# A graph layer on one core: who copies the counts, where the first nodes are kept, one relu for a copied group, and 105 copied groups in place of 104

## The chip, the core and the metric

The kernel runs on one core of a Trainium2 chip. The metric is the device time of one launch in microseconds (us), and lower is better. A core has five engines that run side by side, each through its own instructions in order: PE (matrix products), DVE (vector operations), ACT (activations and copies), POOL (here it only issues gathers) and SP (here it only issues transfers). They wait for each other by semaphores. SBUF is the working memory, PSUM the small memory that PE writes its results to; transfers to and from HBM run on 16 DMA engines.

## The reference

One layer of message passing on a graph with 12,500 nodes of 64 features and 200,000 edges of 32 features, sorted by destination, all in f32:

```python
msg_in = concat([nodes[row], nodes[col], edge_features])       # row: source, col: destination
messages = relu(msg_in @ mW1 + mb1) @ mW2 + mb2
aggregated = segment_sum(messages, col, num_segments=12500)
upd_in = concat([nodes, aggregated])
out = layernorm(x + relu(upd_in @ uW1 + ub1) @ uW2 + ub2)      # over the 64 features
```

## The kernel before

**Tiles, groups, supers, ranges.** A tile is 128 edges; there are 1563. Six tiles are a group `s` (261 of them), two groups a super `g` (131 of them). The edges are sorted, so the destinations of a tile lie in a window of 32 nodes. Groups are gathered into 34 ranges `u` of nodes; for each range PE sums into one PSUM tile `sums` (hidden features of up to 480 nodes) and one PSUM row `cnt` (how many edges each node has, since mb2 enters once for each edge). There are two buffers of `sums`, but one of `cnt`.

**Prologue.** Products of the nodes with the two node parts of mW1 are made once and stored as tables: `tab_a` (source part) and `tab_b` (destination part with mb1).

**One iteration of the main loop** (lines 763 to 831) handles group `s`, with pieces of its neighbours. Its order is written out by hand, and each engine takes its instructions in that order:

- POOL: `gather` (line 217) fetches the source rows of `tab_a` for a later group, 128 rows in one indirect DMA. A buffer `xg` is free again when the add of the group that had it is done; nine are in turn.
- SP: `windows` (lines 276 to 285) reads window starts and fetches rows of `tab_b` into `rhs`.
- `node_part(s)` (line 380): DVE adds the gathered rows to the PSUM tile `pc` (lines 397 and 401), ACT takes the relu (398, 399 and 402) into `h`. `pc` and `h` have two buffers each.
- `joined(s, 0, ...)`: the first part of DVE's column copies (below).
- the update of an earlier range, one stage an iteration: `evacuate` (ACT), `statistics` (DVE), `deviation` (ACT), `norm` (DVE).
- `collect(s - 1)` (line 412): PE adds the counts of the group before (line 431), then its hidden features (line 434). At the first group of a range it first clears `sums` (409) and `cnt` (429).
- `close(u)` (line 445), at the end of a range: ACT copies `cnt` into row 0 of `xw` (line 448) and `sums` into `sums_s` (line 449). PE then reads both: `carry` (442, 443) takes the overlap of 32 nodes over into the next range, `update` (471, 472) makes the node update.
- `select(g + 1)` (line 236), in every second iteration: DVE computes `node` (line 243), the first node of each tile's window against the partition number, into the PSUM tile `cps`; compares the destinations in `l` with it, which turns them into 0 and 1 (line 245); and makes `sel`, a tile's edges against its 32 nodes (line 251). `l` is the weight with which PE spreads the rows of `rhs` over the edges; `cps` also holds `slot`, the numbers 0 to 31.
- `edge_part(s + 1)` (line 363): PE makes `pc` of the next group from `l` and `rhs` (line 374).
- `rest(s)`: pieces of the prologue that are put into the first iterations.
- `joined` again, then `singly` (the column copies on ACT).

**Copied groups.** In 104 of the groups, two of the six tiles are not gathered. Their source columns are instead copied one by one out of `xtop` and `xbot`, which hold all nodes' features, into a tile `xc`: 64 of its 128 columns by ACT (line 345) and 64 by DVE (line 352), at addresses that the engine's sequencer loads eight at a time (line 322). PE then multiplies `xc` with mW1 (line 377). `PACE` (line 74) says how many groups are copied for each group of progress, and so which ones (`COPIED`); the copies of one are spread over the iterations before it, some 26 to 28 columns an iteration on each of the two engines. In a copied group, DVE adds the four gathered tiles from `pc` into `h`, ACT takes their relu in `h`, and a second ACTIVATE takes the relu of the other two tiles straight from `pc`.

`wh`, the input of line 243, is fetched in two parts by `halves` (line 537): the columns of the first eight supers before the loop, the others in `rest(2)`.

Of the kernel before, what the change touches and what calls it, by code (L numbers as in the profile page):

```python
# [10 lines left out]
F32 = mybir.dt.float32  # L11
I32 = mybir.dt.int32
AF = mybir.ActivationFunctionType
ALU = mybir.AluOpType
# [3 lines left out]
P = 128  # L18
# [7 lines left out]
SUP = 12  # L26
NSUP = -(-NT // SUP)
# [3 lines left out]
WIN = 32  # L31
# [15 lines left out]
UW = UN + WIN  # L47
# [23 lines left out]
U8 = mybir.dt.uint8  # L71
YBASE = XBASE + 4 * XCOLS
LEAD = 8
PACE = ((11, 0.413), (50, 0.44), (130, 0.424), (261, 0))
FINAL = 258


def progress(s):

    return sum(r * max(0, min(s + 1, b) - a) for (a, r), (b, _) in zip(PACE, PACE[1:]))  # L80

# [9 lines left out]
def updates():  # L91


    def node(s):
        return N * min(1.0, s * SUB * P / E) ** 2
    at = [0]
    for s in range(1, NSUB):
        if s > at[-1] and node(s + 1) - node(at[-1]) > UN - WIN:
            at.append(s)
    at = [a for a in at if a < NSUB - 32]  # L100
    steps = -(-(NSUB - 3 - at[-1]) // 4)
    return at + [at[-1] + -(-(NSUB - 3 - at[-1]) * (i + 1) // steps) for i in range(steps)]


UPD = updates()

UL = min(UB * P, -(-int(N * (1 - (UPD[-1] * SUB * P / E) ** 2) + WIN // 2) // 64) * 64)


@with_exitstack  # L110
def gnn_kernel(ctx: ExitStack, tc: tile.TileContext, x1T, x, eT, e_rows, src, src_row, dst, dst_row, wlist, wrow, wnext, whalf,
# [24 lines left out]
    nc = tc.nc  # L136
# [21 lines left out]
    xw = [const.tile([P, UB * P], F32, name=f"xw{k}") for k in range(2)]  # L158
# [17 lines left out]
    pidx = const.tile([P, 1], F32, name="pidx")  # L176
# [1 line left out]
    zero_b = const.tile([P, UW], BF, name="zero_b")  # L178

    cpool = ctx.enter_context(tc.tile_pool(name="cpsum", bufs=1, space=bass.MemoryType.PSUM))  # L180
    cps = cpool.tile([P, WIN + SUP], F32, name="cps")
    slot = cps[:, :WIN]
    drc = const.tile([P, NT], F32, name="drc")
    flag_i = const.tile([1, 1], I32, name="flag_i")
# [3 lines left out]
    wh = const.tile([P, NTP // 2], I32, name="wh")  # L188
# [11 lines left out]
    def tiles(s):  # L200
        return range(s * SUB, min((s + 1) * SUB, NT))
# [20 lines left out]
    with tc.tile_pool(name="sup", bufs=2) as sup, tc.tile_pool(name="work", bufs=2) as work, tc.manual_schedule():  # L222
# [3 lines left out]
        def loadd(g):  # L226
# [6 lines left out]
                nc.sync.dma_start(l[q:q + WIN].bitcast(I32), dv[:, b].broadcast_to([WIN, SUP // 2, P]))  # L233
            L[g] = l

        def select(g, at=None):


            nt = min(SUP, NT - g * SUP)
            l = L[g]  # L240
            c = WIN + SUP // 2 * (g % 2)
            node = cps[:, c:c + SUP // 2]
            nc.vector.tensor_scalar(node, wh[:, g * SUP // 2:(g + 1) * SUP // 2], pidx, None, op0=ALU.add)
            for r in ([slice(0, P)] if g > 2 else [slice(q, q + WIN) for q in SK]):
                nc.vector.tensor_tensor(l[r], l[r].bitcast(I32),  # L245
                                        node[r].unsqueeze(2).broadcast_to([r.stop - r.start, SUP // 2, P]),
                                        op=ALU.is_equal)
            if at is not None:
                joined(at, 1, 3)
            s = sup.tile([P, SUP, WIN], F32, name="sel")  # L250
            nc.vector.tensor_tensor(s[:, :nt], slot.unsqueeze(1).broadcast_to([P, nt, WIN]),  # L251
                                    drc[:, g * SUP:g * SUP + nt].unsqueeze(2).broadcast_to([P, nt, WIN]),
                                    op=ALU.is_equal)
            S[g] = s

        def counts(g):

            SB[g] = S[g].bitcast(BF).rearrange("p k (w h) -> p k w h", h=2)
# [88 lines left out]
        def joined(s, part, of):  # L347

            todo = [(o, k, ACTS + e) for o, k, lo, hi in portion(s, P - ACTS) for e in range(lo, hi, 2)]
            for o, k, a, m in share(todo, part, of):  # L350
                for e, top, bot in addresses(k, a, m, ET.DVE):
                    nc.vector.tensor_tensor(o[:, e:e + 1].bitcast(I32), top.bitcast(I32), bot.bitcast(I32),  # L352
                                            op=ALU.bitwise_or)
# [26 lines left out]
        def node_part(s):  # L380

            n = len(tiles(s))
            pc = pcs.pop(s)
            h = work.tile([P, 2, SUB // 2, DH], F32, name="h")
            if s < XG:
                xt = xs.pop(s)
                for i in range(n):
                    k, b = divmod(i, 2)
                    q = 64 * b
                    nc.tensor.matmul(pc[:, b, k, :], xt[q:q + 64, k, :], w1a[q:q + 64], start=False,  # L390
                                     stop=i + 2 >= n)
                nc.scalar.activation(h, pc, AF.Relu)
            else:
                a = xg.pop(s)[0].rearrange("p (b k) f -> p b k f", b=2)
                if s in COPIED:
                    m = SUB // 2 - 1
                    nc.vector.tensor_tensor(h[:, :, :m], pc[:, :, :m], a[:, :, :m], op=ALU.add)  # L397
                    nc.scalar.activation(h[:, :, :m], h[:, :, :m], AF.Relu)  # L398
                    nc.scalar.activation(h[:, :, m:], pc[:, :, m:], AF.Relu)
                for b, m in parts(n) if s not in COPIED else []:  # L400
                    nc.vector.tensor_tensor(h[:, b, :m], pc[:, b, :m], a[:, b, :m], op=ALU.add)  # L401
                    nc.scalar.activation(h[:, b, :m], h[:, b, :m], AF.Relu)  # L402
            hs[s] = h
# [41 lines left out]
        def close(u):  # L445

            ps, pn = sums.pop(u)
            nc.scalar.copy(xw[u % 2][0:1, :UW], pn)
            nc.scalar.copy(sums_s[u % 2], ps)

        us = {}
# [1 line left out]
        def width(u):  # L453

            return UN if u + 1 < K else UL

        def blocks(u):
            return UB if u + 1 < K else -(-UL // P)

# [109 lines left out]
        def zeros(i, n):  # L569

            w = XCOLS // n
            for t in (xtop[D:], xbot[:D]):
                nc.scalar.activation(t[:, i * w:(i + 1) * w], ident[:D, 0:1].broadcast_to([D, w]), AF.Copy, scale=0.0)
# [80 lines left out]
        for k, c in enumerate(range(0, NB, NCH)):  # L654
            chunk_a(c)
            if k == 0:
                chunk_b(0, [B0v, Bv])
            if k == 2:

                w0 = wint[:, :GE * SUP // SUB * LS]  # L660
                nc.vector.tensor_scalar(past, w0[:, GE * SUP // SUB * LS - 1:], float(EARLY - WIN), None, op0=ALU.is_gt)
                nc.vector.tensor_scalar(w0, w0, float(EARLY - WIN), None, op0=ALU.min)
                windows(0)
                windows(1)
            if k == 4:
                relative(0, 8 * SUP)
            if k == 6:
                offsets()
            if k == 9:
                select(0)  # L670
                load(0)
                counts(0)

        def rest(s):

            if 3 <= s < 9 and s % 2:
                others((s - 3) // 2 * 4, (s - 3) // 2 * 4 + 4)
            if 3 <= s < 11:
                zeros(s - 3, 8)
            if s == 9:  # L680
                columns_list()
            if s == 1:
                relative(8 * SUP, 8 * SUP + WCH)
            elif s == 2:
                relative(8 * SUP + WCH, NT)
                halves(4 * SUP, NTP // 2)
            elif s == BS:
                nc.sync.dma_start(wa, wrow.rearrange("o (p c) -> (o p) c", c=NSUP))
                nc.sync.dma_start(wb, wnext.rearrange("o (p c) -> (o p) c", c=NSUP))
                nc.scalar.dma_start(w2, mW2)  # L690
                nc.scalar.dma_start(u1a, uW1[D:2 * D, :])
                nc.scalar.dma_start(b2c, mb2.rearrange("(f o) -> f o", o=1))
                nc.vector.memset(uz[:D], 0.0)
                nc.vector.memset(ux[:D], 0.0)
                nc.vector.memset(eps, EPS)
                nc.vector.memset(ones, 1.0)
                nc.vector.tensor_copy(ux[D:], ident[D:, D:])
                nc.scalar.dma_start(uz[D:], uW1[0:D, :])
                nc.scalar.dma_start(ux[ONE:ONE + 1], ub2.rearrange("(o f) -> o f", o=1))
                nc.scalar.dma_start(ub1_s, ub1.rearrange("(f o) -> f o", o=1))  # L700
                nc.scalar.dma_start(u2, uW2)
            elif s == BS + 2:
                weights()
                checks()
# [14 lines left out]
        def checks():  # L719
# [23 lines left out]
            nc.vector.tensor_scalar(gap[:, :K - 1], gap[:, :K - 1], float(UN), None, op0=ALU.is_gt)  # L743
            nc.vector.tensor_scalar(gap[:, K - 1:K], gap[:, K - 1:K], float(min(UN, UL)), None, op0=ALU.is_gt)
            nc.vector.tensor_copy(gap[:, K:], past)
# [17 lines left out]
        for s in range(last + 2):  # L763
            g, j = divmod(s, SUP // SUB)
# [71 lines left out]
    with tc.If(flag > 0), tc.tile_pool(name="gen", bufs=1) as up:  # L836
# [28 lines left out]
        with tc.For_i(0, NT, 1) as t:  # L865
# [26 lines left out]
            pc = psum.tile([P, DH], F32, name="pcg", tag="pc")  # L892
# [4 lines left out]
            h = up.tile([P, DH], F32, name="hg")  # L897
# [6 lines left out]
            m = up.tile([P, 1], F32, name="m")  # L904
# [97 lines left out]
```

## Time and profile before

| | |
|---|---|
| three runs | 2490.05, 2479.22 and 2493.46 us; median 2490.05 |
| the profiled execution | 2486.88 us, of which the span (first to last instruction) is 2485.1 us |
| clock granted to PE | 0.535 of full speed in the mean |
| DMA | 191.63 MB, mean 77 GB/s |
| 300 to 2440 us of the span: busy | PE 1459.59, DVE 1030.77, ACT 1517.72, POOL 1139.42 us of 2140 |
| gathers (line 217) | 1355, of 944 ns each |
| adds (lines 397, 401) | 104 of 690 ns (four tiles), 146 of 958 ns (six tiles) |

The profile is one execution. A row of a group of instructions gives the line of the kernel, the engine, what is written and read, how many there are, their busy time together and the mean duration of one; then how long the engine sat idle before them, and what ended that: an instruction of another engine, a transfer, "issue" (nothing that the profile shows), or "remote" (a semaphore whose sender it can't tell). The waits are the same idle times, summed by who waited for whom: total, number, longest. Idle time of one engine matters only as far as it delays the end.

### The profile page before, as it was taken

The numbers are of one execution on the slowest core, as the hardware profiler recorded it, in microseconds if no ns is written. First come the engines' busy times: TensorE is split into PE (matmuls) and PEld (weight loads), VectorE is DVE, ScalarE is ACT, GpSimd is POOL, SyncE is SP. The second block draws the span as 40 slices with busy tenths as digits, with TensorE's granted clock in tenths as the row PEclk, the third lists the DMA queues.
The fourth block names the chain that finished last, engine by engine and source line by source line (L and its number), as shares of the span: only waits on it lengthen the run. The fifth ranks groups of instructions, "written<-read, shape, count | busy, mean of one in ns | idle before, by whom it ended". The sixth has DMA issues, their size and how long they took to land. (4 is left out here: it accounts for less than half of the span.)

```text
span 2485.1 us, 47640 instructions
## 1 busy us (share of the span) xinstructions
PE 1630.3 (66%) x9652; PEld 1392.7 (56%) x9652; DVE 1118.3 (45%) x7843; ACT 1612.1 (65%) x7232; POOL 1280.4 (52%) x1364
## 2 busy tenths in 40 slices
PE   1238575666566666666567666776667777777878
PEld 1237465655555555555555555555556656666666
DVE  0211554544444544445444444544544444544544
ACT  0015676767777767768776766776767776777754
POOL 7153455555555555545555555555555555555540
PEclk7565555555555555555555555555555555555556
DMA  5343232322222222222222222222222222222222
GB/s 131 104 120 84 71 91 78 89 78 71 69 67 65 74 64 72 68 68 72 71 71 75 76 69 74 78 75 76 74 75 73 75 78 79 76 77 74 80 72 53
DMA packets 207229, 191.63 MB, mean 77 GB/s; under 512 B 57243, under 2 KB 173297, under 8 KB 206945
## 3 DMA queue, kind: packets, MB, share of 16 engines
q0 software_dynamic: 43360, 86.92, 13.7%
q1 hardware_dynamic: 149040, 92.72, 13.5%
q10 hardware_dynamic: 14546, 8.93, 1.3%
q8 instruction: 91, 1.49, 0.3%
q14 instruction: 192, 1.57, 0.2%
HBM read 170.65 MB, written 17.76 MB: 76 GB/s over the span
## 5 line engine op out<-in xcount | busy, mean ns | idle before, releaser
L217 POOL DMA_INDIRECT xg<-tab_a,src_s x1295 | 1222.6, 944 | 1120.5 <-DVE h L401 403.3
L345 ACT ACTIVATE xc<-xtop,xbot 128x1 f32 x6656 | 1302.3, 281 | 296.7 <-issue 274.0
L352 DVE TENSOR_TENSOR xc<-xtop,xbot 128x1 int32 x6656 | 597.0, 154 | 630.8 <-issue 609.9
L434 PE MATMUL sums<-sel,h 128*128 128x32 f32 x3126 | 688.6, 385 | 140.0 <-issue 82.2
L434 PEld LDWEIGHTS sums<-sel,h 128*128 128x128 f32 x3126 | 655.9, 313 | 168.8 <-issue 82.7
L374 PE MATMUL pc<-rhs,l 64*128 64x128 f32 x3126 | 478.1, 436 | 355.3 <-DVE h L401 85.5
L374 PEld LDWEIGHTS pc<-rhs,l 64*128 64x128 f32 x3126 | 392.2, 309 | 431.7 <-issue 169.0
L245 DVE TENSOR_TENSOR l<-l,cps 128x768 f32<-128x768 int32 (+1 forms) x134 | 127.8, 954 | 167.9 <-remote 84.1
L402 ACT ACTIVATE h<-h 128x768 f32<-128x768 f32 (+1 forms) x148 | 122.5, 829 | 115.0 <-DVE h L401 100.1
L431 PEld LDWEIGHTS <-one 128*1 128x1 bf16 x1563 | 66.1, 83 | 225.0 <-issue 213.4
L431 PE MATMUL cnt<-sel,one 128*1 128x32 bf16 x1563 | 113.2, 188 | 112.8 <-issue 111.7
L401 DVE TENSOR_TENSOR h<-pc,xg 128x768 f32<-128x768 f32 (+1 forms) x148 | 140.4, 949 | 89.5 <-remote 30.4
L397 DVE TENSOR_TENSOR h<-pc,xg 128x512 f32<-128x512 f32 x104 | 71.8, 690 | 183.2 <-remote 71.6
L398 ACT ACTIVATE h<-h 128x512 f32<-128x512 f32 x104 | 64.8, 623 | 106.1 <-DVE h L397 83.4
L251 DVE TENSOR_TENSOR sel<-cps,drc 128x384 f32<-128x384 f32 x131 | 72.0, 549 | 102.0 <-PE sums L434 75.8
L377 PE MATMUL pc<-w1a,xc 64*128 64x128 f32 x416 | 82.9, 398 | 2.0 <-issue 2.0
L590 ACT COPY tb<-pb 128x512 f32<-128x512 f32 (+1 forms) x13 | 7.4, 569 | 114.6 <-remote 74.7
L580 PE MATMUL pb<-w1a,xtop 64*128 64x128 f32 x100 | 25.1, 435 | 84.8 <-DVE tb L588 59.5
L377 PEld LDWEIGHTS pc<-w1a,xc 64*128 64x128 f32 x416 | 73.8, 313 | 2.5 <-issue 2.5
L471 PE MATMUL pu<-xw,uz 128*128 128x448 f32 (+1 forms) x68 | 61.2, 1000 | 18.0 <-DVE h L401 12.4
L493 ACT COPY y<-py 128x256 f32<-128x256 f32 x33 | 12.0, 364 | 93.9 <-remote 67.8
L580 PEld LDWEIGHTS pb<-w1a,xtop 64*128 64x128 f32 x100 | 22.3, 325 | 87.2 <-DVE tb L588 61.3
(104 smaller groups left out, 965.7 us busy)
## 6 DMA issues: line engine op xcount, KB each, us to landing
l<-in_dst_row SPq DMA_DIRECT2D x262, 96.0 KB
l<-in_eT SPq DMA_DIRECT2D x262, 96.0 KB
xg<-tab_a,src_s POOLq DMA_INDIRECT x1295
rhs<-tab_b SPq DMA_DIRECT2D x361, 32.0 KB
tab_b<-tb SPq DMA_DIRECT2D x13, 512.0 KB
rhs<-tab_b SPq DMA_DIRECT2D x387, 16.0 KB
tab_a<-tb ACTq DMA_DIRECT2D x12, 512.0 KB
out<-y SPq DMA_DIRECT2D x33, 128.0 KB
```

What stands on the lines that cost most here:

```text
L217: nc.gpsimd.indirect_dma_start(out=a[:, i, :] if s < XG else a[:, i // 2, i % 2, :], out_offset=None, in_=A[:, :] if s >= XG else x[:, :], ...
L245: nc.vector.tensor_tensor(l[r], l[r].bitcast(I32), node[r].unsqueeze(2).broadcast_to([r.stop - r.start, SUP // 2, P]), op=ALU.is_equal)
L251: nc.vector.tensor_tensor(s[:, :nt], slot.unsqueeze(1).broadcast_to([P, nt, WIN]), drc[:, g * SUP:g * SUP + nt].unsqueeze(2).broadcast_to( ...
L345: nc.scalar.activation(o[:, e:e + 1], top.bitcast(F32), AF.Identity, bias=bot.bitcast(F32))
L352: nc.vector.tensor_tensor(o[:, e:e + 1].bitcast(I32), top.bitcast(I32), bot.bitcast(I32), op=ALU.bitwise_or)
L374: nc.tensor.matmul(pc[:, b, k, :], L[g][q:q + 64, m, :], rhs[g % 2][q:q + 64, w, :], start=s >= XG or k == 0, stop=s >= XG and not copied)
L377: nc.tensor.matmul(pc[:, b, k, :], xc[s][q:q + 64], w1a[q:q + 64], start=False, stop=True)
L397: nc.vector.tensor_tensor(h[:, :, :m], pc[:, :, :m], a[:, :, :m], op=ALU.add)
L401: nc.vector.tensor_tensor(h[:, b, :m], pc[:, b, :m], a[:, b, :m], op=ALU.add)
L402: nc.scalar.activation(h[:, b, :m], h[:, b, :m], AF.Relu)
L431: nc.tensor.matmul(pn[:, bass.ds(ws[i], WIN)], one, SB[g][:, k0 + i, :, 1], start=False, stop=ends and i == n - 1)
L434: nc.tensor.matmul(ps[:, bass.ds(ws[i], WIN)], h[:, i % 2, i // 2, :], S[g][:, k0 + i, :], start=False, stop=ends and i == n - 1)
```

## The change

- `close`: DVE copies the counts, in place of ACT. The copy of `sums` stays on ACT.
- `cps` grows from 44 to 512 columns (one PSUM bank of 2 KB), and holds the first nodes of 80 supers, six columns each. Three calls of the new `first_nodes` fill them: for supers 0 to 7 ahead of the first `select`, for 8 to 79 in iteration 6, and for 80 to 130, over the first ones, in iteration 157. `select` no longer computes its own.
- Copied groups: the add writes back into `pc`, in PSUM, and one ACTIVATE takes the relu of all six tiles from `pc` into `h`.
- `PACE`: slightly higher rates, by which 105 groups are copied and most of them move by a group or so.

```diff
-PACE = ((11, 0.413), (50, 0.44), (130, 0.424), (261, 0))
+PACE = ((11, 0.42), (50, 0.446), (130, 0.429), (261, 0))
...
+NODES = 80
...
-    cps = cpool.tile([P, WIN + SUP], F32, name="cps")
+    cps = cpool.tile([P, WIN + NODES * SUP // 2], F32, name="cps")
...
+        def first_nodes(a, b):
+
+            c = WIN + SUP // 2 * (a % NODES)
+            nc.vector.tensor_scalar(cps[:, c:c + SUP // 2 * (b - a)], wh[:, SUP // 2 * a:SUP // 2 * b], pidx, None, op0=ALU.add)
+
         def select(g, at=None):
...
-            c = WIN + SUP // 2 * (g % 2)
+            c = WIN + SUP // 2 * (g % NODES)
             node = cps[:, c:c + SUP // 2]
-            nc.vector.tensor_scalar(node, wh[:, g * SUP // 2:(g + 1) * SUP // 2], pidx, None, op0=ALU.add)
...
                 if s in COPIED:
                     m = SUB // 2 - 1
-                    nc.vector.tensor_tensor(h[:, :, :m], pc[:, :, :m], a[:, :, :m], op=ALU.add)
-                    nc.scalar.activation(h[:, :, :m], h[:, :, :m], AF.Relu)
-                    nc.scalar.activation(h[:, :, m:], pc[:, :, m:], AF.Relu)
+                    nc.vector.tensor_tensor(pc[:, :, :m], pc[:, :, :m], a[:, :, :m], op=ALU.add)
+                    nc.scalar.activation(h, pc, AF.Relu)
...
             ps, pn = sums.pop(u)
-            nc.scalar.copy(xw[u % 2][0:1, :UW], pn)
+            nc.vector.tensor_copy(xw[u % 2][0:1, :UW], pn)
             nc.scalar.copy(sums_s[u % 2], ps)
...
             if k == 9:
+                first_nodes(0, 8)
                 select(0)
...
+            if s == 6:
+                first_nodes(8, NODES)
+            if s == 2 * NODES - 3:
+                first_nodes(NODES, NSUP)
```

## The prediction

> **What bounds the kernel now.** I read the page's busy times first, then the waits, then the groups of instructions, then a stretch of the timeline. The page's chain covers only the last 80 us or so, so it says nothing of the middle.
>
> ```profile
> PE 1630.3 (66%) x9652; PEld 1392.7 (56%) x9652; DVE 1118.3 (45%) x7843; ACT 1612.1 (65%) x7232; POOL 1280.4 (52%) x1364
> ```
>
> No engine is full. The waits of the whole run say what fills the rest:
>
> ```profile
> DVE xc L352 <- issue: 609.9, 1061, 1.8
> POOL xg L217 <- DVE h L401: 403.3, 110, 13.1
> ...
> ACT xc L345 <- issue: 274.0, 446, 1.8
> POOL xg L217 <- DVE h L397: 248.9, 76, 8.3
> ...
> PE cnt L429 <- remote: 27.4, 4, 8.7
> ...
> PE cnt L429 <- ACT xw L448: 22.8, 8, 8.7
> ```
>
> POOL waits 652 us for adds that free its buffers; by the trace a group's last gather ends about 70 us before its add. POOL is not the bound. "issue" before a column copy is the engine's own time (the address loads of L322). Counted so over 300 to 2440 us, an engine's own time (busy, plus idle with nothing to wait for) is ACT 1820 us (85%), PE 1739 (81%), DVE 1735 (81%); for each other they wait 319, 399 and 406 us. Three engines in lockstep, none much ahead: a group of six tiles takes (2440 - 300)/237, about 9.0 us. So I count a microsecond added to or taken from one of the three at **one third**, with 0 and 1 as the ends.
>
> ```profile
> L345 ACT ACTIVATE xc<-xtop,xbot 128x1 f32 x6656 | 1302.3, 281 | 296.7 <-issue 274.0 <-DMA ub_s<-in_ub 17.0
> ...
> L352 DVE TENSOR_TENSOR xc<-xtop,xbot 128x1 int32 x6656 | 597.0, 154 | 630.8 <-issue 609.9 <-DMA xg<-tab_a,src_s 4.3
> ...
> L398 ACT ACTIVATE h<-h 128x512 f32<-128x512 f32 x104 | 64.8, 623 | 106.1 <-DVE h L397 83.4 <-remote 13.4 <-issue 9.2
> ...
> L399 ACT ACTIVATE h<-pc 128x256 f32<-128x256 f32 x104 | 38.0, 366 | 1.8 <-issue 1.4
> ...
> L243 DVE TENSOR_SCALAR cps<-wh,pidx 128x6 f32<-128x6 int32 x131 | 28.8, 220 | 6.9 <-issue 6.8
> ...
> L448 ACT COPY xw<-cnt 1x480 f32<-1x480 f32 x34 | 18.2, 534 | 18.9 <-remote 18.3 <-PE cnt L431 0.5
> ...
> L588 DVE COPY tb<-pb 128x512 f32<-128x512 f32 x12 | 8.3, 689 | 64.5 <-ACT tb L590 58.8 <-issue 5.7
> ...
> L392 ACT ACTIVATE h<-pc 128x768 f32<-128x768 f32 x10 | 8.0, 803 | 24.9 <-remote 13.6 <-PE pc L390 4.6 <-PE sums L434 4.0
> ```
>
> These rows price every edit. The timeline around one closing shows the places (start, duration, engine, line; in brackets the idle time before):
>
> ```profile
> 1446.04 0.63 ACT L398 ACTIVATE h<-h 128x512 f32<-128x512 f32 x1 [1.75 <-DVE h L397]
> ...
> 1446.58 0.36 ACT L399 ACTIVATE h<-pc 128x256 f32<-128x256 f32 x1
> ...
> 1449.78 0.23 DVE L243 TENSOR_SCALAR cps<-wh,pidx 128x6 f32<-128x6 int32 x1 [1.51 <-issue]
> ...
> 1453.68 0.55 ACT L448 COPY xw<-cnt 1x480 f32<-1x480 f32 x1 [6.74 <-remote]
> 1453.69 0.95 DVE L245 TENSOR_TENSOR l<-l,cps 128x768 f32<-128x768 int32 x1 [3.68 <-remote]
> ...
> 1454.28 0.56 PE L429 MATMUL cnt<-zero_b 128*1 128x480 bf16 x1 [8.72 <-ACT xw L448]
> ```
>
> The next range's first count matmul waits for ACT's copy, since there is one count buffer. This is also one of some sixty stretches, 640 us together, in which PE, DVE, ACT and SP each issue an instruction only every 0.7 us or so; in the trace they begin five or six gathers into an unbroken run of POOL's and end when it ends.
>
> **Part 1, first nodes (DVE).** 131 of L243 go. From its start to that of the compare behind it is 0.25 us where the compare follows at once; in the trace that is 75 of 131, and in 56 the compare waits for something else (a landing of l above all), which hides L243. Gain 75 x 0.25 = 18.8 us. Added are three wide ones of 48, 432 and 306 elements. The nearest row is L243 itself with 6, and DVE's slope between the 512- and the 768-element adds (690, 958 ns) is 1.05 ns an element: 0.26 + 0.67 + 0.54 = 1.5 us. Their input wh is issued by 136 us, and iteration 6 stands at 192 us, so nothing waits. DVE: -17.3 us.
>
> **Part 2, the count copy moves.** ACT loses 34 copies. Start to start, L448 to L449 is 0.44 us in 24 closings; in the other ten L449 waits for the sums anyway, and nothing is gained. ACT: 24 x 0.44 = -10.5 us (at most 34 x 0.534 = 18.2). DVE gains 34 copies of 480 elements out of PSUM: by L588, 689 - 32 x 1.05 = 0.66 us, 22.3 us in all. One partition instead of 128 saves nothing: on ACT 534 against 547 ns. The counts stand ahead of the sums on PE, so they are done: here the last ended at 1440.8, and DVE would come to the copy at 1448.3. Behind the copy on DVE stand select's compare (PE's L374 of the next super waits for its l), the column copies and the next add; these wait 0.66 us. PE's wait at L429 changes too. I put DVE's place (end of its first column copies, plus 0.66 us) beside the end of ACT's copy at each closing: where PE waited, eleven closings come earlier, 25 us in all, 16 of them at three closings in slow stretches where DVE is slow as well; seven come later, 7 us. PE: about -17 us (ends -25 and +7).
>
> **Part 3, one relu.** A copied group has L398 and L399, 0.90 us from the first's start to the second's end in the median; one ACTIVATE 128x768 from PSUM is L392, 0.80 us. 104 x 0.10 = -10.2 us (by the rows' means, 0.989 - 0.803, -19.3). The sums of the first four tiles start 0.18 us later, those of the last two and the release of pc 0.1 us earlier: nothing net. The add now writes PSUM. No row has an add that does. The nearest, the cast of slot into cps (32 elements, 196 ns), against ux<-ident in SBUF (64 elements, 192 ns), leaves 10 to 40 ns for the place. [...]
>
> [...]
>
> **Part 4, one more copied group.** One group more is (1302.3 + 274.0)/104 = 15.2 us of ACT, (597.0 + 609.9)/104 = 11.6 us of DVE and four matmuls of some 0.2 us on PE; two gathers go, hidden by the 70 us of lead. Its add is 0.27 us shorter. One long run of gathers less is worth about 1 us of slow stretch (268 us of ACT's idle in them over 157 groups of six gathers).
>
> **Part 5, fewer instructions.** ACT has 34 + 104 - 64 - 8 = 66 fewer, address loads counted, DVE about 22 fewer. In the slow stretches (30% of the 2140 us) one costs about 0.45 us more than elsewhere: 66 x 0.3 x 0.45 = 9 us of ACT, 3 us of DVE, not in the rows above.
>
> **The sum.** DVE -17.3 + 22.3 + 11.6 - 0.3 - 3 = +13.3; ACT -10.5 - 10.2 + 15.2 - 9 = -14.5; PE -17 + 0.8 = -16.2. A third of each: +4.4 - 4.8 - 5.4, and -1 for the gathers: **-6.8 us**. The profiled execution took 2486.9 us (span 2485.1), so 2480; the median of the three runs is 3.2 us above it, so I forecast 2490.05 - 6.8 = **2483 us**. Half a per cent, 12.5 us, is about what a measurement of this kernel can tell from no change: its three runs spread over 14.2 us.
>
> **The rivals.**
> - **ACT is the bound** (85% of its own time, the most of the three): its sum counts in full and at the rows' means, -18.2 - 19.3 + 15.2, -22 us, and with part 5 -31. I take the middle, about -25: **2465 us**. For: POOL and PE end up waiting for adds, and ACT's column copies stand ahead of each relu. Against: ACT itself waits 183 us for adds.
> - **DVE becomes the bound**, slower. The copy and the twelfth of column copies stand ahead of select's compare and the next add, and adds release POOL, ACT and PE alike (PE's L374 and POOL have them as first releasers). It decides once DVE's own 1735 us, +16 us without part 5, runs into PE's waits; with part 1's 17 us hidden as well in select's waits, +16 to +33. I take +18: **2508 us**. Against: DVE waits 406 us.
> - **Nothing reaches the end**: the edits only shift waits between the three, and the slow stretches, set by gathers, stay. **2490 us**, give or take 3.
> - That the change doesn't do what it says is only so in part: 56 of 131 removed L243 were hidden already. It is in the sum.
>
> **Chances.** Forecast (2475 to 2489) 0.43; ACT 0.30; nothing 0.13; DVE 0.14. Range: 2464 to 2506, from ACT's middle to just short of DVE's. Faster by over 0.5% (below 2477.6): nearly all of ACT's, a fifth of the forecast's, 0.38. Slower by over 0.5% (above 2502.5): 0.13. Within: 0.49.
>
> **What would show it.** L243 gone but for three rows (0.3 to 0.7 us); the DVE copy at 0.62 to 0.70 us x34; one ACTIVATE 128x768 x105 at 0.80 in place of L398 and L399; the add at 0.67 to 0.76; idle before PE's L429 down from 54 us to under 40; ACT's busy time down some 25 us (-18.2 - 19.3 + 12.5), DVE's within 3 us of now (-28.8 + 1.5 + 22.3 + 5.7 - 0.3). Wrong if the add into PSUM takes over 0.8 us, if PE waits longer at L429 because DVE comes late, or if the 640 us of slow stretches change by more than 10 us: I have no model of their start beyond the runs of gathers.

## The result, and the profile after

The changed kernel takes 2459.03 us in the median of four runs (2450.92 to 2461.25), the kernel before 2487.25 us beside it (four runs). The ratio is 0.9882 [0.9844, 0.992]: 1.2% faster, some 29 us where 6.8 were forecast, and below the range. The profiled execution of the changed kernel took 2450.92 us (span 2449.1).

Busy times first; by the page of the profile after, hardly one has moved:

```profile
PE 1612.1 (66%) x9656; PEld 1381.8 (56%) x9656; DVE 1125.1 (46%) x7813; ACT 1603.2 (65%) x7158; POOL 1278.5 (52%) x1362
```

ACT is 9 us less busy, DVE 7 us more, PE 18 us less. The span is 36 us shorter, so most of the gain lies in idle time. The largest waits of the run after are together no shorter than before; "issue" before DVE's column copies has even grown, from 609.9 to 701.8 us, and POOL waits for adds nearly as long (652 us before, 640 after):

```profile
DVE xc L357 <- issue: 701.8, 1140, 2.1
POOL xg L218 <- DVE h L405: 427.7, 115, 13.4
...
ACT xc L350 <- issue: 319.7, 511, 2.1
POOL xg L218 <- DVE pc L402: 212.4, 67, 7.0
```

The groups of instructions show the row that did shrink. L250 is the old L245 (the compare), L240 the old L243, L402 and L403 the add and the one relu, L452 the count copy, L433 the old L429:

```profile
L250 DVE TENSOR_TENSOR l<-l,cps 128x768 f32<-128x768 int32 (+1 forms) x134 | 127.2, 949 | 67.9 <-DMA l<-in_dst_row 51.5 <-issue 15.9
L403 ACT ACTIVATE h<-pc 128x768 f32<-128x768 f32 x105 | 84.1, 801 | 103.0 <-DVE pc L402 84.3 <-issue 8.4 <-remote 7.8
L402 DVE TENSOR_TENSOR pc<-pc,xg 128x512 f32<-128x512 f32 x105 | 73.4, 699 | 146.4 <-remote 57.9 <-PE pc L379 41.5 <-PE sums L438 25.0
L452 DVE COPY xw<-cnt 1x480 f32<-1x480 f32 x34 | 21.6, 634 | 10.4 <-remote 8.7 <-issue 1.7
L433 PE MATMUL cnt<-zero_b 128*1 128x480 bf16 x34 | 18.6, 547 | 81.2 <-DVE xw L452 47.4 <-remote 12.0 <-issue 11.2
L240 DVE TENSOR_SCALAR cps<-wh,pidx 128x48 f32<-128x48 int32 (+2 forms) x3 | 1.4, 478 | 0.0
```

The prices were forecast well: relu 801 ns (0.80), add 699 (0.67 to 0.76), copy 634 (0.62 to 0.70), the wide first nodes 1.4 us (1.5). What nobody had priced is the compare. Its row of before, and what it waited for:

```profile
L245 DVE TENSOR_TENSOR l<-l,cps 128x768 f32<-128x768 int32 (+1 forms) x134 | 127.8, 954 | 167.9 <-remote 84.1 <-DMA l<-in_dst_row 51.5 <-issue 25.4
```

```profile
DVE l L245 <- remote: 84.1, 19, 7.6
DVE l L245 <- DMA l<-in_dst_row: 51.5, 20, 5.6
DVE l L245 <- issue: 25.4, 10, 6.1
...
DVE l L245 <- DVE cps L243: 4.2, 7, 1.1
```

These are the prediction's 56 waiting compares (19 + 20 + 10 + 7). The landings of `l` are as large after as before, 51.5 us. The 84.1 us put down to "remote" are gone. A "remote" releaser is a semaphore whose sender the profile can't tell, and the timeline of before shows who it was. At 1853.66 us, as at 1449.78 in the stretch that the prediction shows, L243 has ended and the compare, which is the next instruction on the same engine and reads what L243 wrote, starts 5.51 us later:

```profile
1852.76 0.98 DVE L517 TENSOR_SCALAR y<-y,mv,rs 128x64 f32<-128x64 f32 x4 [3.40 <-remote]
1853.66 0.22 DVE L243 TENSOR_SCALAR cps<-wh,pidx 128x6 f32<-128x6 int32 x1
1859.39 0.95 DVE L245 TENSOR_TENSOR l<-l,cps 128x768 f32<-128x768 int32 x1 [5.51 <-remote]
```

In the trace's records at 1449.78, L243 ends at 1450.01, the semaphore that it raises is recorded as raised at 1453.67, and the compare, which waits for that semaphore, starts at 1453.69. So the update came 3.66 us after the instruction's end, and the profile, which looks for a sender near the update, found none. The other 18 "remote" waits are alike: each ends with an update of DVE's own semaphore, some 24 ns before the compare starts, and L243 is the last DVE instruction before it.

How common late updates are, the trace tells only in part. From the end of an instruction to the next record of its semaphore the median is 12 ns, and 471 of DVE's 1281 instructions show more than 0.5 us. But the trace holds only 938 such records, so an instruction can have lost its own and show a later one's. For L243 the two can be told apart: of its 131 updates 62 seem late, and in 38 of these the compare had started before the record, so the update can't have been that late. The other 24 stay. Of these, 20 fall where PE, DVE, ACT and SP together start fewer than eight instructions a microsecond (over 2 us), of the remaining 107 only five: the late updates lie in the slow stretches.

### The profile page after: what moved, and what is told of

Read it like the earlier page. It is cut to its first block, busy times and chain, and to the rows that moved or that the text cites. A ratio compares the mean times of both kernels' runs of the same rounds, so it can differ in the third digit from the quotient of the medians.

```text
span 2449.1 us, 47549 instructions
## 1 busy us (share of the span) xinstructions
PE 1612.1 (66%) x9656; PEld 1381.8 (56%) x9656; DVE 1125.1 (46%) x7813; ACT 1603.2 (65%) x7158; POOL 1278.5 (52%) x1362
## 4 chain that ended last, share of the span: by engine, by line
issue 27%; PE 18%; ACT 12%; DVE 12%; POOL 12%; another core or an unknown queue 8%; DMA 3%; DVEq 3%; ACTq 2%; SPq 1%; POOLq 0%
POOL xg L218 12%; ACT xc L350 10%; PE sums L438 7%; DVE xc L357 6%; PE pc L379 6%; DVEq L327 3%; DVE h L405 2%; ACTq L327 2%; PE py L489 1%; PE py L491 1%; DVE pc L402 1%; DVE l L250 1%; SPq L287 1%; DMA xg<-tab_a,src_s 1%
## 5 line engine op out<-in xcount | busy, mean ns | idle before, releaser
L350 ACT ACTIVATE xc<-xtop,xbot 128x1 f32 x6720 | 1321.7, 281 | 342.4 <-issue 319.7
L357 DVE TENSOR_TENSOR xc<-xtop,xbot 128x1 int32 x6720 | 608.5, 154 | 723.1 <-issue 701.8
L406 ACT ACTIVATE h<-h 128x768 f32<-128x768 f32 x147 | 121.7, 828 | 83.9 <-DVE h L405 76.5
L405 DVE TENSOR_TENSOR h<-pc,xg 128x768 f32<-128x768 f32 x147 | 139.4, 949 | 65.8 <-PE pc L379 18.8
L250 DVE TENSOR_TENSOR l<-l,cps 128x768 f32<-128x768 int32 (+1 forms) x134 | 127.2, 949 | 67.9 <-DMA l<-in_dst_row 51.5
L403 ACT ACTIVATE h<-pc 128x768 f32<-128x768 f32 x105 | 84.1, 801 | 103.0 <-DVE pc L402 84.3
L402 DVE TENSOR_TENSOR pc<-pc,xg 128x512 f32<-128x512 f32 x105 | 73.4, 699 | 146.4 <-remote 57.9
L382 PE MATMUL pc<-w1a,xc 64*128 64x128 f32 x420 | 89.5, 405 | 6.9 <-issue 6.9
L489 PE MATMUL py<-ux,xw 128*128 128x64 f32 x268 | 62.4, 410 | 27.3 <-remote 22.1
L489 PEld LDWEIGHTS py<-ux,xw 128*128 128x128 f32 x268 | 56.6, 311 | 34.9 <-remote 23.0
L433 PE MATMUL cnt<-zero_b 128*1 128x480 bf16 x34 | 18.6, 547 | 81.2 <-DVE xw L452 47.4
```

What stands on the lines that cost most here:

```text
L250: nc.vector.tensor_tensor(l[r], l[r].bitcast(I32), node[r].unsqueeze(2).broadcast_to([r.stop - r.start, SUP // 2, P]), op=ALU.is_equal)
L350: nc.scalar.activation(o[:, e:e + 1], top.bitcast(F32), AF.Identity, bias=bot.bitcast(F32))
L382: nc.tensor.matmul(pc[:, b, k, :], xc[s][q:q + 64], w1a[q:q + 64], start=False, stop=True)
L489: nc.tensor.matmul(py[:, i], xw[u % 2][:, i * P:(i + 1) * P], ux, start=i == 0, stop=False)
```

## The theories

**Late updates (T).** In the slow stretches a semaphore is raised microseconds after its instruction ended (3.66 us at 1449.78). An instruction that waits for the one just ahead of it on its own engine has nothing else to do meanwhile. The compare was such an instruction; part 1 took the wait away, not merely 0.22 us of work. Parts 2 to 4 are worth nothing together.

**Rivals.** (a) DVE's own time: what counts is the 28.8 us of L243 that are gone. (b) ACT is the bound: the gain is that of parts 2 and 3. (c) Any edit shifts the collisions and moves the time by a per cent; nothing in particular caused it.

## Experiments

Every kernel was timed in five rounds beside the kernel before on the same chip. Three chips came up, and they differ: on chips A and C the kernel before takes 2479 to 2494 us, as in the comparison above; on chip B it takes 1715.45 us. Ratios are within one chip.

### Each part by itself (chip A)

Part 1 alone is the change's `first_nodes`, `NODES` and `cps` on the kernel before:

```diff
-            nc.vector.tensor_scalar(node, wh[:, g * SUP // 2:(g + 1) * SUP // 2], pidx, None, op0=ALU.add)
...
+            if s == 6:
+                first_nodes(8, NODES)
```

> The kernel before with the first nodes kept in PSUM and nothing else of the change. Late-update theory (in the slow stretches a semaphore update arrives microseconds after the instruction that makes it, so the compare, which waits on the update of line 243 just ahead of it, stands 84 us in all; with the nodes made long before, that wait is gone): 18 to 35 us faster (0.7 to 1.4%), the compare's idle time down from 168 to about 70 us. ACT theory (ACT is the bound, and the saving comes from its copies and relus): at most 7 us faster. DVE-time theory (DVE is the bound and each of its instructions counts in full): 19 to 29 us faster, by the busy time alone.

Measured: **0.9902 [0.9871, 0.9932]**. The one relu alone (the diff's lines of the copied group) and the count copy alone (the diff's line in `close`):

> The kernel before with the add into PSUM and one relu for all six tiles of a copied group, and nothing else. Late-update theory: within 6 us of before (10 us of ACT at a third, one wait for one wait). ACT theory: 10 to 20 us faster. DVE-time theory: within 3 us of before (add 690 to 700 ns).

Measured: 1.002 [0.9995, 1.0045].

> The kernel before with the counts copied by DVE, and nothing else. Late-update theory: from 6 us faster to 6 us slower, since PE's wait for the count buffer at line 429 is made of late updates that DVE's copy sends as late as ACT's did. ACT theory: 10 to 18 us faster. DVE-time theory: 15 to 22 us slower.

Measured: 1.0049 [1.0026, 1.0072], slower by some 12 us; T had allowed 6, so its range was missed, and the theory of DVE's own time came nearer with 15 to 22. Part 1 alone gives the whole gain within the intervals, and the two edits that relieve ACT give none, so rival (b) falls. These runs don't yet part the wait from the work, since part 1 removes both.

### The first nodes one super ahead (chip A, not a clean test)

```diff
-            c = WIN + SUP // 2 * (g % 2)
+            c = WIN + SUP // 2 * (g % 4)
...
             S[g] = s
+            if g + 1 < NSUP:
+                first_nodes(g + 1)
```

> The kernel before, with line 243 kept once a super (131 instructions, none saved), but issued one super earlier, behind sel of the super before, into one of four slots. Late-update theory: most of the gain of the first nodes is here too, 10 to 30 us faster, and the compare's wait for an unknown sender goes from 84 us to under 15. DVE-time theory: within 4 us of before, since DVE does the same instructions. ACT theory: within 4 us of before.

Measured: 1.0075 [1.0046, 1.0103], slower, against T. The groups of this kernel (L239 the first nodes, L249 the compare, L255 `sel`):

```profile
L249 DVE TENSOR_TENSOR l<-l,cps 128x768 f32<-128x768 int32 (+1 forms) x134 | 127.3, 950 | 68.6 <-DMA l<-in_dst_row 42.5 <-issue 24.8
L255 DVE TENSOR_TENSOR sel<-cps,drc 128x384 f32<-128x384 f32 x131 | 72.0, 549 | 125.0 <-PE sums L440 73.7 <-remote 47.8 <-issue 1.7
...
L239 DVE TENSOR_SCALAR cps<-wh,pidx 128x6 f32<-128x6 int32 x131 | 29.7, 227 | 28.7 <-remote 20.6 <-DVE sel L255 3.9
```

The compare's unknown sender is gone, as T expected, but a part of the wait was moved rather than removed: `sel` reads `cps` too, so L239 now waits for `sel`, the instruction just ahead of it (20.6 + 3.9 us of the 84). The 47.8 us of "remote" before `sel` (15.9 in the kernel before) are of another kind: in the trace all 15 end with an update of PE's semaphore, and the kernels with the whole gain have 28 us and more of them too. By T this kernel should have kept most of the gain. Why it is slower than before, and not faster, stays open.

### The wait apart from the work

Three kernels part T from rival (a). `nodes_plus_op` is part 1 alone with an instruction of L243's size put back right ahead of each compare, whose result nobody reads. `nodes_plus_wait` is part 1 alone (with room for 78 supers in place of 80) with a 59 ns memset there instead, into a spare column of `cps`, so that the compare waits again for its neighbour. `four_slots` is the kernel before with four slots for the first nodes, which should change nothing.

```diff
+            nc.vector.tensor_scalar(spare[g % 4], wh[:, g * SUP // 2:(g + 1) * SUP // 2], pidx, None, op0=ALU.add)
```
```diff
+            nc.vector.memset(cps[:, WIN + NODES * SUP // 2 + g % 4:][:, :1], 0.0)
```
```diff
-    cps = cpool.tile([P, WIN + SUP], F32, name="cps")
+    cps = cpool.tile([P, WIN + 2 * SUP], F32, name="cps")
...
-            c = WIN + SUP // 2 * (g % 2)
+            c = WIN + SUP // 2 * (g % 4)
```

They first ran on chip B, with the change without part 1 beside them:

> The first nodes alone (0.990 of before), and in front of each compare an operation of line 243's form that writes a spare tile in SBUF: DVE does the same 131 operations in the same places as before, but the compare waits for none of them. Late-update theory: the gain stays, ratio 0.988 to 0.996. DVE-time theory: the gain is gone, 0.997 to 1.003. If the one before (an order that gave up the wait but was 0.75% slower) only shows that any edit shifts the time by as much, this lands anywhere between 0.985 and 1.008.

> The first nodes alone, and in front of each compare a memset of one spare column of cps (some 59 ns), for which the compare has to wait as it had to for line 243: little work, but the wait. Late-update theory: the gain is gone, 0.996 to 1.004, and the compare again stands some 84 us for an unknown sender. DVE-time theory: three quarters of the gain stay (the operation is a quarter as long), 0.990 to 0.994.

> The kernel before with the first nodes of a super in one of four places of cps instead of two: no instruction, wait or order differs. All theories: 0.998 to 1.002. If it is further off, so far can a kernel's time move by an edit that does nothing, and a single result of this size says nothing.

> The whole change without the first nodes: count copy on DVE, one relu, 105 copied groups. Late-update theory: the gain of 1.2% is the first nodes' (0.990 alone), so 0.996 to 1.006. ACT theory: 0.985 to 0.992. DVE-time theory: 1.003 to 1.010.

Measured on chip B: 0.999 [0.9982, 0.9999], 0.9997 [0.9986, 1.0007], 0.9995 [0.9986, 1.0004], and 1.0111 [1.0095, 1.0126] without part 1, above the range of every theory. The first two tell nothing between T and (a), because on this chip there are no slow stretches: by the count of instructions started, as above, 1.9 us in the first of them and none in the others. POOL's gathers run on in one row, 1.25 us apart, as the timeline of `four_slots` shows, and POOL is never idle for more than 0.32 us between two of them:

```profile
800.06 0.95 POOL L217 DMA_INDIRECT xg<-tab_a,src_s  x1 [0.30 <-issue]
801.31 0.94 POOL L217 DMA_INDIRECT xg<-tab_a,src_s  x1 [0.30 <-issue]
802.56 0.95 POOL L217 DMA_INDIRECT xg<-tab_a,src_s  x1 [0.30 <-issue]
```

```profile
POOL xg L217 <- issue: 376.2, 1234, 0.3
```

So all 1355 gathers follow each other from 2.8 to 1696.9 us of a span of 1711.0 us. But for the last 14 us the gathers fill this kernel's time, and neither DVE's work nor its waits can show much in it. Without part 1 the gathers end as early, at 1694.5 us, but the other engines need 41 us more instead of 14. Of L243's updates 8 seem over 0.5 us late in `four_slots`, and in all 8 the compare had started before the record: none is shown to be late. The compare of `nodes_plus_wait`, with its wait for the memset, stands idle mostly for landings, and 0.3 us for the memset:

```profile
L252 DVE TENSOR_TENSOR l<-l,cps 128x768 f32<-128x768 int32 (+1 forms) x134 | 127.8, 954 | 21.4 <-DMA l<-in_dst_row 16.5 <-DVE cps L250 0.3
```

On chip B, then, 0.3 us of idle time is put down to 131 such waits.

The same three, and the changed kernel again, on chip C:

> The first nodes kept in PSUM, and in their place, right before every compare, an instruction of the same engine, size and duration (0.25 us) that writes a spare tile for which nobody waits: the instruction count and VectorE's own time are those of the kernel before, only the compare's wait for the instruction just ahead of it is gone. If this kernel runs in some 2,480 us here (the chip on which the gathers come in stretches): the late-update theory (the 84 us were the wait) expects 0.988 to 0.996 and the compare's idle time at some 70 us with no unknown sender in it; the theory that each VectorE instruction counts by its own time expects 0.998 to 1.004. If it runs in some 1,715 us here, both expect 0.997 to 1.001, as no wait is late there.

> The first nodes kept in PSUM, and in their place a 59 ns memset of a spare column of the tile that the compare reads, right ahead of each compare, so that the compare waits again for the instruction just ahead of it. At some 2,480 us: the late-update theory expects the wait back (idle of 60 to 110 us at the compare with an unknown sender) and a ratio of 0.996 to 1.004; the theory of VectorE's own time expects 0.990 to 0.994, since 100 times 0.19 us of work are still gone. At some 1,715 us: 0.999 to 1.001 by both.

> The kernel before with four slots in place of two for the first nodes' tile and nothing else: no instruction less, no wait less. By both theories 0.997 to 1.003; what it shows beyond that is how far an edit that should do nothing moves the time.

> The changed kernel once more, for its ratio beside the three others. At some 2,480 us: 0.984 to 0.992, of which the late-update theory gives nearly all to the first nodes. At some 1,715 us, where the first nodes are worth nothing: 1.005 to 1.012, as the three other parts gave by themselves there.

Measured on chip C: with the work put back **0.9896 [0.9864, 0.9928]**; with the wait put back **0.999 [0.9967, 1.0012]**; four slots 0.9975 [0.9951, 0.9998]; the changed kernel 0.9908 [0.9873, 0.9943]. The compare's row in the first two:

```profile
L253 DVE TENSOR_TENSOR l<-l,cps 128x768 f32<-128x768 int32 (+1 forms) x134 | 127.1, 949 | 74.7 <-DMA l<-in_dst_row 52.5 <-issue 22.1
```

```profile
L252 DVE TENSOR_TENSOR l<-l,cps 128x768 f32<-128x768 int32 (+1 forms) x134 | 127.8, 954 | 146.7 <-remote 73.4 <-DMA l<-in_dst_row 55.9 <-issue 8.9
```

Read the two together. The first keeps all of L243's work (131 x 232 ns) and loses the wait: the gain is whole. The second has taken away 21 us of that work (28.8 to 7.7 us) and keeps a wait: the unknown sender is back with 73.4 us, and the gain is gone. This is T's outcome, inside its ranges, and outside those of (a), which expected 0.998 to 1.004 and 0.990 to 0.994. By the trace all 18 of the second's "remote" waits end with an update of DVE's semaphore, with the memset as the last DVE instruction before it.

The size of the wait is less certain than 84.1 us suggests. `four_slots`, which keeps L243 as it was, has 54.2 us of it on this chip:

```profile
L245 DVE TENSOR_TENSOR l<-l,cps 128x768 f32<-128x768 int32 (+1 forms) x134 | 127.8, 954 | 128.3 <-remote 54.2 <-DMA l<-in_dst_row 53.0 <-issue 10.3
```

The one relu alone has 111.5 us. Six profiles with the neighbour's wait give 54 to 112 us, those without it next to none.

The pair doesn't part everything. The work put back writes SBUF, while L243 and the memset write `cps`, in PSUM. By the ratios alone, the time could as well hang on DVE's write into `cps` in every super: the kernels that have it, `nodes_ahead` included, lie at 0.9975 and above, those without it at 0.9908 and below. No row shows a price of such a write (220 ns for L243, 232 ns for the same work into SBUF), and the trace names the semaphore that the compare waited for; that speaks for T. But a wait of this kind on an SBUF tile, or a write into `cps` without any such wait, was not tried at the compare.

Against (c): the four slots, an edit that should do nothing, move the time by some 0.25%. Of the twelve ratios on chips A and C, the first comparison included (three of them come below), the six without the neighbour's wait lie from 0.987 to 0.9908 and the five with it from 0.9975 to 1.0049. Only `nodes_ahead`, where some 25 of the 84 us were moved, stands outside, and its unexplained 0.75% says how much else an edit can move.

### The other three parts where there are stretches, and another wait of the kind (chip A)

`inverse_ahead` is part 1 alone, and in a range's last stage it issues the reciprocal ahead of the group's column copies, so that the first normalising instruction doesn't stand right behind it:

```diff
+            if earlier(5) is not None:
+                inverse(earlier(5))
             if s < NSUB:
                 node_part(s)
```

> The change without its first nodes: the count copy on VectorE, the one relu, the 105th copied group. At some 2,480 us: the late-update theory gives the first nodes the whole gain and so expects 0.996 to 1.004 here; the theory that VectorE's own time counts (22 us of copies and 12 of column copies added) expects 1.002 to 1.008; the theory that ScalarE is the bound expects 0.988 to 0.994. At some 1,715 us: 1.009 to 1.013 again.

> The first nodes alone, again, as the measure beside which the two others are read. At some 2,480 us 0.986 to 0.994 by the late-update theory; at some 1,715 us 0.998 to 1.001.

> The first nodes alone, and with them the next wait of the same kind taken away: the reciprocal of a range's deviations is issued ahead of the group's column copies, so that the first normalising instruction no longer stands right behind the reciprocal that it reads. No instruction is added or removed. At some 2,480 us: the late-update theory, if it holds for every wait on the instruction just ahead and not for the compare's alone, expects the idle time ahead of the normalising instruction to fall from some 40 us to under 12, and by the share that the compare's idle time gave (24 to 26 us of time for 84 to 100 us of idle time) some 8 to 12 us less than the first nodes alone, 0.982 to 0.988; the rival that the compare's place alone mattered expects the ratio of the first nodes alone. At some 1,715 us: no difference from the first nodes alone beyond 0.001.

Measured: without part 1 1.0013 [0.9983, 1.0042]; part 1 alone 0.9886 [0.9846, 0.9925]; with the reciprocal ahead **0.987 [0.983, 0.991]** (2450.03 us against 2457.82, with intervals that overlap). Parts 2 to 4 are worth nothing that can be measured here. The normalising instruction's row, part 1 alone and then with the reciprocal ahead:

```profile
L523 DVE TENSOR_SCALAR y<-y,mv,rs 128x64 f32<-128x64 f32 x132 | 33.8, 324 | 34.7 <-remote 22.6 <-issue 6.8 <-DVE rs L520 4.5
```

```profile
L530 DVE TENSOR_SCALAR y<-y,mv,rs 128x64 f32<-128x64 f32 x132 | 33.8, 334 | 8.9 <-issue 8.8
```

The wait itself vanishes like the compare's, so it doesn't belong to the compare's place alone; and the reciprocal writes `rs` in SBUF, so neither does it belong to PSUM alone. Whether its 26 us (34.7 - 8.9) shorten the run isn't settled: the 7.8 us are little more than the 6 us by which the four slots, which should do nothing, moved the time, and the ratio 0.987 is inside the range of the rival too.

## Why the prediction was wrong

- **Part 1 is the step that failed**: "in 56 the compare waits for something else (a landing of l above all), which hides L243". Landings were 20 of the 56 and 51.5 of 165 us. The 19 "remote" ones, 84.1 us, were L243's own late updates, which hid nothing: they were part 1's to remove. The prediction's timeline showed one of them, 3.68 us between L243's end and the compare. At its own weight of a third, these 84 us would have added 28 us and given some 2455 us; the 54 us of `four_slots` would have given 2465.
- **The weight of a third** can be checked only roughly for that idle time. Taking the wait away but not the work removed 1.04%, 26 us. Against the first comparison's profile 93 us of idle time before the compare went with it (167.9 - 74.7), a weight of 0.28; against `four_slots` on the same chip 54 us (128.3 - 74.7), a weight of about a half. Part of the rest came back as "issue" before DVE's column copies: 609.9 us before and 621.4 with four slots, 658.5 in that kernel, 701.8 after the change. L243's own work, at 5.8 us in the sum, is below what these runs can part: 0.9896 with it, 0.9902 and 0.9886 without it.
- **Part 2, PE's -17 us, was not there.** PE's idle time at the first count matmul (54.0 us, 34 closings) did not fall under 40: 81.2 after, with 47.4 for the DVE copy. But it is 54.6 in the profile of the same change on chip C, and with ACT's copy it is 61.8 us with the work put back and 81.1 with the one relu alone. Thirty-four waits read closing by closing in one execution don't carry to the next. On chip B the wait for the DVE copy is 36.8 us in place of 6.0 for ACT's, and the time rises by 1.1%; that this wait is the cause there was not tried by itself.
- **Part 3** was priced rightly (relu 801 ns), and gained nothing: 1.002 alone. The sum has no term for the add's place; into PSUM it took 699 ns against 690 into SBUF, and no run shows an add near the 0.76 us that was its upper end. ACT's terms were real and reached no end. ACT's busy time fell by 9 us, not 25.
- **Parts 2 to 5 together** were put at -1.0 us by the sum (-6.8 + 5.8); measured without part 1, 1.0013 [0.9983, 1.0042], -4 to +10 us. The sum holds as a whole, not term by term.
- **Rivals.** "ACT is the bound" gave 2465 us, near the time measured, by a cause that the runs exclude. "DVE becomes the bound" shows in the copy alone on chip A (+12 us) and in parts 2 to 4 on chip B (+20 us), its sign at least; the whole change doesn't show it where there are stretches, since part 1 outweighs it.
- **A test that tells nothing.** The prediction called itself wrong if the slow stretches changed by more than 10 us. Counted from the traces by the rule used above for the late updates, from 300 us on and without the last 45 us, which is narrower than the 640, they are 423 us before and 437 after while the time fell, 429 in the kernel with the work put back and 405 with the reciprocal ahead. Their total doesn't follow the time.

What stays open: why `nodes_ahead` is slower; whether the wait alone, or also the write into `cps`, costs the time; what makes updates late (in the trace they go with the stretches, which go with unbroken runs of gathers; that the gathers cause it was not tried, and chip B has the longest run of all, 1355 gathers, without any of it); and what distinguishes chip B.

## What to carry to other kernels

Before a wait is called cover for a removed instruction, ask whose semaphore it is: a "remote" wait just behind an instruction of the same engine, whose output the waiter reads, may be that instruction's own late update, and then removing it can be worth a share of the wait (here some 26 us for 54 to 93 us of idle time), and not its duration. To tell work from wait, put the work back without the dependence, and the dependence back without the work, both into the same memory. Where chips differ as much as here, an edit is worth what it is worth on each: of these versions, part 1 alone is at 0.99 where there are stretches, and with its work kept costs nothing on the other chip; parts 2 to 4 cost 1.1% there and give nothing here.

## What the runs showed of the hardware that was not expected

- The kernel before takes 1715 us on one chip and 2479 to 2494 us on two others, while the busy times differ far less: with four slots on chip B ACT 1548.2 us and PE 1459.2, against 1612.1 and 1630.3 in the profile of before. On chip B ACT is busy for 90% of the span, and the gathers run unbroken through 99% of it:

```profile
PE 1459.2 (85%) x9652; PEld 1259.0 (74%) x9652; DVE 1099.3 (64%) x7843; ACT 1548.2 (90%) x7232; POOL 1282.4 (75%) x1364
```

- The granted clock doesn't explain it: in the mean 0.583 on chip B and 0.536 on chip C for the kernel with four slots, 9% apart where the times are 45% apart.
- A semaphore's update came 3.66 and 5.5 us after its instruction's recorded end in the two cases above, so that the compare's wait for the instruction ahead of it on its own engine took longer than that instruction (220 ns): 84 us at 19 of 131 compares. In the profile of `four_slots` on chip B none of L243's updates is shown to be late.
- The 128x512 add on DVE took 699 ns writing PSUM (after) and 690 writing SBUF (before).
